# Graph kernel with rows gathered one tile at a time: the first four chunks of the first convolution gather raw rows of x in the prologue

## The chip, the cores and the metric

The kernel runs on one core of a Trainium2 chip. The metric is the time of one execution on the device in microseconds (us). Before the change three runs gave 4202.74, 4210.86 and 4212.08, so the median is 4210.86 us. The profile is of a further execution of the same kernel.

## What is computed

The reference normalizes the rows of x (12,500 rows of 256 numbers), runs two graph convolutions over 200,000 edges sorted by their destination, adds the result to x, and then runs an attention layer (its edges' first 12,500 only). What matters here is the first convolution:

```python
edge_index = jnp.stack([src, dst])
h = jnp.maximum(_layernorm(x, axis=-1), 0.0)
...
    h = x @ W_pre + b_pre
    h = _gcn_conv(h, W1, b1, src, dst, n)      # with a loop added at each node
...
    deg = jax.ops.segment_sum(ones, dst, num_segments=n)
    dinv = jnp.where(deg > 0, jax.lax.rsqrt(deg), 0.0)
    norm = dinv[src] * dinv[dst]
    msgs = h[src] * norm[:, None]
    out = jax.ops.segment_sum(msgs, dst, num_segments=n)
```

So each edge takes the row of its source, normalized and multiplied by the source's dinv, and adds it to its destination. The linear maps are applied after the sums.

## The kernel before

All of it is in `fast_path` (L414 on). Instructions stand on each engine in the order of the program, and each engine works through its own queue in that order; a buffer that is used again brings a wait for its last reader.

**The prologue** (L518 to L925) has three jobs. It counts the edges of each node on TensorE (16 blocks s = 0 to 15 in the loop at L862; `count_block` L764 makes one-hots `hot_r` on VectorE, `place` L782 and `norms` L817 turn the counts of one of five parts into `dinv`). It turns the edge lists (`turn_to`, `turn_src`). And it makes table1 in DRAM, 14 groups of 7 tiles of 128 rows: `load_x` (L575) loads a group of x on SP's queue, `stats` (L751) takes its means and variances on VectorE, and `scale(g)` (L828) multiplies the factors with four small GpSimd instructions (L834 to L837), normalizes the seven tiles on ScalarE (L846, in the last two groups partly on VectorE, L842 and L844) and stores the group to table1 (L848, SP's queue). All 14 groups have a buffer each: 11 are loaded at once, and 3 when the edge lists' memory is given back after s = 2. `scale(g)` is put into the loop when the `dinv` of its part is there.

**The first convolution** is `convolve` (L986), called at L1247. The edges are cut into 112 chunks of 14 tiles of 128 edges (the last chunk has 9 tiles): 1,563 tiles. Per tile GpSimd issues one indirect DMA that gathers 128 rows of table1 into a slice of `fgot` (L1179), and TensorE multiplies the tile with a one-hot of the destinations (L1187; two matmul instructions in the profile per tile). Per chunk VectorE makes the one-hots (`fhot`, L1073), ScalarE copies the sums out (L1103), TensorE turns them (L1038), and VectorE adds them to a sliding buffer (L1120). Finished windows of 128 nodes go through the combined weight (L1220, L1221), ScalarE (L1225) and a store to table2 (L1226). `fgot` has four buffers, so GpSimd may be four chunks ahead of TensorE. A list of due steps (`at`, `run`) places the later steps between the tiles: the first finished window ends at tile 50, in chunk 3, and brings with it `load_late` (L970), `first_chunk` (L959) and `check_chunks` (L933), whose instructions on VectorE and TensorE stand there in the queues.

**The second convolution** (L1392) does the same with table2. Its first chunk gathers from all of table2 but the last two windows (`some`, L1178), and those two are added by other means (`late_sums` L1083). Then comes **the attention** (L1399 on).

Of the kernel before, what the change touches and what calls it, by code (L numbers as in the profile page):

```python
# [413 lines left out]
def fast_path(  # L414
# [102 lines left out]

    with tc.tile_pool(name="fprep", bufs=1) as prep:  # L518
# [42 lines left out]

        dst_r = load_edges(dst, NOWHERE, "fdst_r")

# [9 lines left out]
        xs = []  # L573

        def load_x(g, pool):  # L575
            n0, n1 = g * G * P, min((g + 1) * G * P, N)

            xt = pool.tile([P, G, D1], F32, name="fxt", bufs=XB if g < XB else NG - XB)
# [10 lines left out]
        XB = 11  # L589
        for g in range(XB):  # L590
            load_x(g, prep)
            if g == 1:
                src_r = load_edges(src, 0, "fsrc_r")


        zeros = prep.tile([1, 512], BF16, name="zeros")
# [11 lines left out]
        for k in range(NPT):  # L608
# [4 lines left out]
        iota_a = prep.tile([I, L, max(AW)], BF16, name="iota_a")  # L613
        nc.gpsimd.iota(iota_a, pattern=[[0, L], [1, max(AW)]], base=0, channel_multiplier=0,
                       allow_small_or_imprecise_dtypes=True)


        sel = prep.tile([2 * R, P // LB, P], F32, name="sel")
        nc.gpsimd.memset(sel, 0.0)
        for r0, base, keep in ((0, 0, [-1, LB - 1]), (R, LB, [1, -LB])):  # L620
            s = sel[r0:r0 + R]
            nc.gpsimd.affine_select(out=s, in_=s, compare_op=ALU.not_equal, fill=1.0, base=base,
# [20 lines left out]
        for k, q in enumerate(Q):  # L643
            nc.gpsimd.tensor_mul(low_q[k], low[:, :, None].to_broadcast([NCH, J, q]),
                                 by_kq[:, k, None, :q].to_broadcast([NCH, J, q]))
        base = prep.tile([NCH, 1], F32, name="base")
        nc.vector.tensor_copy(base, dst_r[:, 0:1])
        near_t = prep.tile([P, J, NCH], BF16, name="near_t")
# [6 lines left out]
        def offsets():  # L655


            mean = prep.tile([NCH, 1], F32, name="fmean")
            nc.gpsimd.iota(mean, pattern=[[0, 1]], base=-LAG, channel_multiplier=M,
                           allow_small_or_imprecise_dtypes=True)  # L660
            nc.gpsimd.tensor_scalar(mean, mean, 0.0, None, op0=ALU.max)
            mean_i = prep.tile([NCH, 1], I32, name="mean_i")
            nc.gpsimd.tensor_copy(mean_i, mean)
            nc.vector.tensor_scalar(mean_i, mean_i, ~(P - 1), None, op0=ALU.bitwise_and)
# [39 lines left out]
        with tc.tile_pool(name="fpsum", bufs=2, space=PSUM) as psum, \  # L704
# [28 lines left out]
            def turn_to():  # L733
                to_f = rows_p.tile([NCH, CE], F32, name="fto_f")
# [3 lines left out]
            def turn_src():  # L738
                src_f = rows_p.tile([NCH, CE], F32, name="near_f")
# [42 lines left out]
            def place(k):  # L782
# [4 lines left out]
                hot = prep.tile([I, L * max(AW)], BF16, name="hot_n", bufs=2)  # L787
# [39 lines left out]

            def scale(both):  # L828
# [4 lines left out]
                flip(g)  # L833
                nc.gpsimd.tensor_mul(sc[:, ws], sc[:, ws], dinv[:, ws])  # L834
# [21 lines left out]
            def one_more():  # L856
                nonlocal n_stats
                if n_stats < NG:
                    stats(n_stats)
                    n_stats += 1  # L860

            for s, (k, j0) in enumerate(blocks):  # L862
                count_block(k, j0)
                if to_scale and to_scale[0] + 1 < n_stats:
# [15 lines left out]
                if s == 2:  # L880
# [3 lines left out]
                    for g in range(XB, NG):  # L884
                        load_x(g, more)
            place(late)
            due.append((len(blocks), late))
# [6 lines left out]
            while to_scale:  # L894
                scale(True)
            nc.vector.reciprocal(dinv2, deg)
# [36 lines left out]
    def check_chunks(work, psum):  # L933
# [9 lines left out]
        pt = psum.tile([P, KC + 1, P], F32, name="fpt", bufs=1)  # L943
# [42 lines left out]
    def convolve(ep, table, stride, width, ahead, with_sum, psum, prepare, finish, lacking=False):  # L986
# [95 lines left out]

        def late_sums():  # L1083
# [3 lines left out]
            froms = ep.tile([P, J, stride], F32, name="fgot", bufs=ahead)  # L1087
# [81 lines left out]
        hots = {0: hot_of(0)}  # L1169
# [377 lines left out]
```

## Time and profile before

| what | us |
|---|---|
| median of three runs | 4210.86 |
| the profiled execution: its time | 4207.15 |
| its span, from the first to the last instruction | 4205.4 |
| prologue: start to GpSimd's first gather from table1 | 0 to 124.5 |
| first convolution's gathers (1,563) | 124.5 to 2079.2 |
| second convolution's gathers (1,563) | 2082.4 to 4040.6 |
| attention, to the end | 4040.6 to 4205.4 |

In a row of the page's groups the name before the arrow is what is written and the name behind it what is read; then come the count, the busy time, the mean of one in ns, and the idle time of that engine just before, with what ended most of it. A row of the timeline has the start, the duration, the engine, the line and operation, and in brackets the idle time before it. In a row of waits, the engine and its line come first, then what it waited for, and then the total, the number and the longest wait. The GpSimd engine is called POOL, VectorE DVE, ScalarE ACT, TensorE PE; "issue" is time in which the engine waited for nothing that the profile shows.

### The profile page before, as it was taken

Reading aid. Unit: us, or ns where it says so; the run is one execution under the profiler, and the core shown is the slowest. Engines: PE = TensorE matmul, PEld = TensorE weight load, DVE = VectorE, ACT = ScalarE, POOL = GpSimd, SP = SyncE. Lnnn points to the kernel's source line nnn. Section 1 sums busy time; section 2 is a strip of 40 time slices with the busy share of each in tenths; the row PEclk is TensorE's granted clock in tenths of the full one; section 3 lists DMA queues with packets and bytes.
Section 4 is the critical chain, followed back from the end, with each engine's and each line's share of the span. In section 5 each row is a group of like instructions: output and inputs, shape, how many; then the busy total and the mean of one; then the engine's idle time right before and its main releaser. Section 6 shows DMA issues by size and latency. Waiting matters only on the chain. (4 is left out here: it accounts for less than half of the span.)

```text
span 4205.4 us, 31693 instructions
## 1 busy us (share of the span) xinstructions
PE 3105.7 (74%) x10423; PEld 1964.0 (47%) x10423; DVE 1098.5 (26%) x2260; ACT 459.4 (11%) x1155; POOL 3101.1 (74%) x3346
## 2 busy tenths in 40 slices
PE   6488878788787877888667777777677677777773
PEld 5254434444444444444355555555455445545552
DVE  7321111211111112111132222222222222222238
ACT  5100000000000000000001111111111111111122
POOL 3677777777777777777777777777777777777766
PEclk7687787877877778777788888888888888788877
DMA  6544444444444444444445554545555545555556
GB/s 220 156 122 120 120 120 122 120 120 120 122 119 119 119 122 119 120 119 121 128 137 140 130 127 127 132 127 128 128 132 128 128 127 132 127 127 127 132 159 203
DMA packets 326197, 551.36 MB, mean 131 GB/s; under 512 B 96041, under 2 KB 224520, under 8 KB 326024
## 3 DMA queue, kind: packets, MB, share of 16 engines
q0 software_dynamic: 153520, 414.27, 38.3%
q1 hardware_dynamic: 126966, 118.80, 9.5%
q10 hardware_dynamic: 45538, 16.17, 1.5%
q8 instruction: 86, 1.41, 0.1%
q14 instruction: 87, 0.71, 0.1%
HBM read 495.73 MB, written 53.19 MB: 131 GB/s over the span
## 5 line engine op out<-in xcount | busy, mean ns | idle before, releaser
L1179 POOL DMA_INDIRECT fgot<-ftable,fsrc_t x3112 | 2945.8, 947 | 957.2 <-issue 899.6
L1187 PE MATMUL facc<-fgot,fhot 128*128 128x257 f32 (+1 forms) x6252 | 2368.0, 499 | 912.8 <-DMA fgot<-ftable,fsrc_t 879.7
L1187 PEld LDWEIGHTS facc<-fgot,fhot 128*128 128x128 f32 x6252 | 1269.0, 233 | 1850.8 <-DMA fgot<-ftable,fsrc_t 1395.6
L1120 DVE TENSOR_TENSOR buf<-buf,fturn 128x256 f32 x224 | 94.4, 422 | 1722.9 <-PE fturn L1038 1354.3
L1073 DVE TENSOR_TENSOR fhot<-iota_p,to_t 128x1792 f32<-128x1792 f32 x224 | 448.6, 2004 | 4.3 <-PE fpt L1094 4.3
L1276 DVE SCALAR_TENSOR_TENSOR fy<-rb,fb2c,fpz 128x128 f32<-128x128 f32 x194 | 58.7, 344 | 752.3 <-PE fpz L1269 751.3
L1103 ACT ACTIVATE fsums<-facc 128x257 f32<-128x257 f32 (+1 forms) x224 | 86.1, 384 | 1236.5 <-PE facc L1187 1228.9
L1290 DVE SCALAR_TENSOR_TENSOR fx<-fpo,fdinv,fxb 128x256 f32<-128x256 f32 x97 | 46.9, 483 | 471.8 <-PE fpo L1285 471.8
L1220 PE MATMUL fpo<-wf,buf 128*128 128x256 f32 x388 | 157.1, 549 | 0.4 <-DVE buf L1120 0.4
L1225 ACT ACTIVATE fo<-fpo,fdinv 128x256 f32<-128x256 f32 x97 | 46.0, 474 | 784.9 <-PE fpo L1221 784.9
L1220 PEld LDWEIGHTS fpo<-wf,buf 128*128 128x128 f32 x388 | 115.5, 298 | 30.2 <-DVE buf L1120 0.7
L1269 PE MATMUL fpz<-buf,fwb 128*128 128x128 f32 x776 | 122.8, 310 | 0.0
L1269 PEld LDWEIGHTS fpz<-buf,fwb 128*128 128x128 f32 x776 | 120.1, 233 | 2.2 <-DVE fy L1276 0.3
L1038 PE MATMUL fturn<-fident,self 128*128 128x128 f32 x396 | 85.9, 303 | 40.0 <-DMA self<-ftable 36.4
L1285 PE MATMUL fpo<-fwo,fz 128*128 128x256 f32 x388 | 115.3, 423 | 0.0
L1456 POOL DMA_INDIRECT fal<-table_l,fsrc_t x84 | 81.7, 972 | 25.6 <-issue 22.9
L1038 PE MATMUL fturn<-fident,fsums 128*128 128x128 f32 x448 | 96.7, 302 | 0.5 <-ACT fsums L1103 0.5
L1446 PE MATMUL fends<-rows,hot_t 128*128 128x260 f32 x168 | 61.3, 511 | 42.7 <-ACT fxg L1448 40.5
L1315 ACT ACTIVATE ht<-fpt 128x256 f32<-128x256 f32 x97 | 37.3, 384 | 476.3 <-PE fpt L1311 476.3
L1221 PE MATMUL fpo<-bb,fins 2*128 2x256 f32 x194 | 85.7, 528 | 0.0
L1038 PEld LDWEIGHTS fturn<-fident,fsums 128*128 128x128 f32 x448 | 70.8, 158 | 31.6 <-issue 8.6
L1038 PEld LDWEIGHTS fturn<-fident,self 128*128 128x128 f32 x396 | 56.8, 160 | 48.3 <-issue 38.3
(225 smaller groups left out, 1555.1 us busy)
## 6 DMA issues: line engine op xcount, KB each, us to landing
fgot<-ftable,fsrc_t POOLq DMA_INDIRECT x3112, 2.8
ftable<-fxt SPq DMA_DIRECT2D x14, 910.0 KB
self<-ftable SPq DMA_DIRECT2D x99, 128.0 KB
self<-ftable SPq DMA_DIRECT2D x97, 130.0 KB
ftable<-fo ACTq DMA_DIRECT2D x98, 128.0 KB
kept_x<-fx SPq DMA_DIRECT2D x98, 128.0 KB
fxb<-in_x_dram SPq DMA_DIRECT2D x97, 128.0 KB
fxt<-in_x_dram SPq DMA_DIRECT2D x13, 896.0 KB
```

The source lines that it names most:

```text
L1038: nc.tensor.transpose(v["pt"][:, i * KC + k, :], rows[:, k * P:(k + 1) * P], ident)
L1073: nc.vector.tensor_tensor(h, iota_p[:, None, :].to_broadcast([P, n, P]), to[:, :, None].to_broadcast([P, n, P]), ALU.is_equal)
L1103: nc.scalar.activation(sb, acc, AF.Copy)
L1120: nc.vector.tensor_add(b, b, v["pt"][:, :KC, :])
L1179: nc.gpsimd.indirect_dma_start(out=got, out_offset=None, in_=table[:(NT - TW) * P, :] if some else table[:], in_offset=bass.IndirectOffset ...
L1187: nc.tensor.matmul(acc, hots[c][:, j, :], got[:, :width], start=(j == 0), stop=(j == nj[c] - 1 and not some))
L1220: nc.tensor.matmul(po, buf[:, k, :P], wf[:, k, :], start=(k == 0), stop=False)
L1221: nc.tensor.matmul(po, fs, bb, start=False, stop=True)
L1269: nc.tensor.matmul(pz[:, m, :], wb[:, k, m * P:(m + 1) * P], buf[:, k, :P], start=(k == 0), stop=(k == KC - 1))
L1285: nc.tensor.matmul(po, v["z"][:, m, :], wo[:, m, :], start=(m == 0), stop=(m == KC - 1))
L1446: nc.tensor.matmul(px, hot_t[c][:, j * P:(j + 1) * P], rows[c], start=True, stop=True)
L1456: nc.gpsimd.indirect_dma_start(out=al[:, i, :], out_offset=None, in_=(table_l if c else table_e)[:], in_offset=bass.IndirectOffsetOnAxis(a ...
```

## The change

The first four chunks of the first convolution no longer gather from table1. Their 56 gathers take raw rows of x and stand in the prologue's GpSimd queue: four, then two, then three after each block s = 0 to 15 (`fetch`). For that the first 7,168 source numbers are loaded and turned ahead of everything else, and they are split into a low and a high part and stored to DRAM (`lohi`). The four chunks are normalized in place in their `fgot` buffers: `raw_stats` takes the statistics of the 14 tiles, `raw_sources` finds the dinv of each row's source by products of one-hots with dinv (as three bf16 parts), and `raw_scaled` applies both with ScalarE. Chunk 0 is done at the end of the prologue, chunks 1 to 3 inside `convolve`, each between the chunk before it and its own matmuls (`raw_begin` at tile 3 of the chunk before, `raw_end` after its close).

The `fgot` buffers of the first convolution are five instead of four, in a pool that is opened ahead of the prologue: four hold the raw chunks, and chunk 4 is the first to gather from table1. To make room, x passes through seven buffers instead of 14: `refill` in `scale(g)`, g = 1 to 7, loads group g + 6 into the buffer of group g - 1, and its GpSimd memset stands ahead of the four GpSimd instructions of `scale(g)`. Smaller moves: `mean` is computed earlier, `sel` in two halves after blocks 1 and 2, and in the second convolution the pool with its `fgot` is opened after the work pool, so that it lies elsewhere. The attention's early tiles (`ap`) are allocated after the first convolution instead of before it.

```diff
@@ -515,6 +515,76 @@
...
+    RAW = 4
...
+    lohi = dram.tile([2, KR, P], BF16, name="lohi")
...
+    ring = ctx.enter_context(ExitStack())
+    gp = ring.enter_context(tc.tile_pool(name="fgots", bufs=1))
+    d_src = gp.tile([P, KR], F32, name="d_src")
+    raw_mv = gp.tile([P, KR, 2], F32, name="raw_mv")
+    raw_sc = gp.tile([P, KR], F32, name="raw_sc")
+    raw_st = gp.tile([P, J, 6], F32, name="raw_st")
+    parts_d = gp.tile([P, 3, NT], BF16, name="parts_d")
...
+    def new_got():
+        return gp.tile([P, J, D1], F32, name="fgot", bufs=RAW + 1)
+
+    raw = [new_got() for c in range(RAW)]
...
+    def raw_stats(c):
+
+        for j in range(J):
+            nc.vector.bn_stats(raw_st[:, j, :], raw[c][:, j, :D])
+        for j in range(J):
+            nc.vector.bn_aggr(raw_mv[:, c * J + j, :], raw_st[:, j, :])
+        k = slice(c * J, (c + 1) * J)
+        nc.scalar.activation(raw_sc[:, k], raw_mv[:, k, 1], AF.Sqrt, bias=eps)
...
+    def raw_ends(c, both):
+
+        lo, hi = both[:, :CE], both[:NT, CE:2 * CE]
+        for v, n, i in ((lo, P, 0), (hi, NT, 1)):
+            nc.sync.dma_start(v, lohi[i, c * J:(c + 1) * J, :].rearrange(
+                "t p -> (t p)").partition_broadcast(n))
+        return lo, hi
...
+    def raw_hots(ends):
+        nc.vector.tensor_scalar(ends[0], ends[0], lane, None, op0=ALU.is_equal)
+
+    def raw_sources(c, ends, m, new_psum):
+
+        lo, hi = ends
+        for j0 in range(0, J, 4):
+            j1 = min(j0 + 4, J)
+            e = slice(j0 * P, j1 * P)
+            pt = new_psum()[:NT, :(j1 - j0) * P]
+            for i in range(3):
+                nc.tensor.matmul(pt, parts_d[:, i, :], lo[:, e], start=(i == 0), stop=(i == 2))
+            nc.vector.scalar_tensor_tensor(m[:NT, e], hi[:, e], lane[:NT], pt,
+                                           op0=ALU.is_equal, op1=ALU.mult)
+        pd = new_psum()[:, :J]
+        for j in range(J):
+            nc.tensor.matmul(pd[:, j:j + 1], m[:NT, j * P:(j + 1) * P], one, start=True,
+                             stop=True)
+        nc.vector.tensor_copy(d_src[:, c * J:(c + 1) * J], pd)
...
+    def raw_scaled(c):
+
+        k = slice(c * J, (c + 1) * J)
+        nc.vector.reciprocal(raw_sc[:, k], raw_sc[:, k])
+        nc.vector.tensor_mul(raw_sc[:, k], raw_sc[:, k], d_src[:, k])
+        nc.vector.scalar_tensor_tensor(raw_mv[:, k, 0], raw_mv[:, k, 0], -1.0, raw_sc[:, k],
+                                       op0=ALU.mult, op1=ALU.mult)
+        nc.vector.tensor_copy(raw[c][:, :, D], d_src[:, k])
+        for j in range(J):
+            v = raw[c][:, j, :D]
+            i = c * J + j
+            nc.scalar.activation(v, v, AF.Relu, bias=raw_mv[:, i, 0:1], scale=raw_sc[:, i:i + 1])
...
+        early_t = rows_p.tile([KR, 5 * P], F32, name="early")
+        early_i = early_t.bitcast(I32)
+        src_e, lo_e, hi_e = (early_i[:KR, i * P:(i + 1) * P] for i in range(3))
+        nc.scalar.dma_start(src_e, src[:KR * P].rearrange("(t p) -> t p", p=P))
...
+        nc.vector.tensor_copy(src_ef, src_e)
+        raw_i = prep.tile([P, KR], I32, name="raw_i")
+        with tc.tile_pool(name="epsum", bufs=1, space=PSUM) as psum:
+            pe = psum.tile([P, KR], F32, name="fe")
+            nc.tensor.transpose(pe, src_ef, ident[:KR, :KR])
+            nc.vector.tensor_copy(raw_i, pe)
...
+        nc.scalar.dma_start(lohi.rearrange("i t p -> t i p"), early_b)
...
+        def fetch(n):
+            nonlocal fetched
+            for k in range(fetched, min(fetched + n, KR)):
+                c, j = divmod(k, J)
+                nc.gpsimd.indirect_dma_start(
+                    out=raw[c][:, j, :D], out_offset=None, in_=x[:],
+                    in_offset=bass.IndirectOffsetOnAxis(ap=raw_i[:, k:k + 1], axis=0))
+            fetched = min(fetched + n, KR)
...
@@ -571,11 +671,15 @@
...
         xs = []
-
-        def load_x(g, pool):
+        XB, XM = 4, 3
+
+        def load_x():
+            g = len(xs)
             n0, n1 = g * G * P, min((g + 1) * G * P, N)
 
-            xt = pool.tile([P, G, D1], F32, name="fxt", bufs=XB if g < XB else NG - XB)
+            low = g % (XB + XM) < XB
+            pool = prep if low else more
+            xt = pool.tile([P, G, D1], F32, name="fxt", bufs=XB if low else XM)
...
-        XB = 11
         for g in range(XB):
-            load_x(g, prep)
+            load_x()
...
+        mean = prep.tile([NCH, 1], F32, name="fmean")
+        nc.gpsimd.iota(mean, pattern=[[0, 1]], base=-LAG, channel_multiplier=M,
                        allow_small_or_imprecise_dtypes=True)
+        nc.gpsimd.tensor_scalar(mean, mean, 0.0, None, op0=ALU.max)
+        mean_i = prep.tile([NCH, 1], I32, name="mean_i")
+        nc.gpsimd.tensor_copy(mean_i, mean)
+        fetch(4)
...
+        def selects(r0, base, keep):
             s = sel[r0:r0 + R]
+            nc.gpsimd.memset(s, 0.0)
...
+        nc.vector.tensor_scalar(mean_i, mean_i, ~(P - 1), None, op0=ALU.bitwise_and)
+        fetch(2)
...
@@ -825,12 +935,19 @@
 
...
+            def refill(g):
+                if XB + XM <= len(xs) < NG:
+                    assert len(xs) < g + XB + XM
+                    load_x()
+
             def scale(both):
 
                 g = to_scale.pop(0)
                 t = xs[g]
                 ws = slice(g * G, (g + 1) * G)
                 flip(g)
+                if g:
+                    refill(g)
...
             for s, (k, j0) in enumerate(blocks):
                 count_block(k, j0)
+                if s in (1, 2):
+                    selects(*((0, 0, [-1, LB - 1]), (R, LB, [1, -LB]))[s - 1])
                 if to_scale and to_scale[0] + 1 < n_stats:
                     scale(False)
                 if s % 2 == 0:
@@ -881,9 +1000,13 @@
                     turn_src()
                     edges.close()
                     more = edges.enter_context(tc.tile_pool(name="fmore", bufs=1))
-                    for g in range(XB, NG):
-                        load_x(g, more)
+                    for g in range(XM):
+                        load_x()
+                fetch(3)
             place(late)
+            fetch(KR)
+            lohi_0 = raw_ends(0, prep.tile([P, R * BLOCK], BF16, name="hot_r", bufs=2))
+            raw_stats(0)
...
@@ -893,6 +1016,17 @@
                     norms(due.pop(0)[1])
             while to_scale:
                 scale(True)
+
+            rest = prep.tile([P, NT], F32, name="fdeg2")
+            nc.vector.tensor_copy(parts_d[:, 0, :], dinv)
+            nc.vector.tensor_sub(rest, dinv, parts_d[:, 0, :])
+            nc.vector.tensor_copy(parts_d[:, 1, :], rest)
+            nc.vector.tensor_sub(rest, rest, parts_d[:, 1, :])
+            nc.vector.tensor_copy(parts_d[:, 2, :], rest)
+            raw_hots(lohi_0)
+            raw_sources(0, lohi_0, iota_r.rearrange("p r b -> p (r b)").bitcast(F32),
+                        lambda: psum.tile([P, 4 * P], F32, name="ft"))
+            raw_scaled(0)
             nc.vector.reciprocal(dinv2, deg)
         edges.close()
...
@@ -1167,19 +1307,44 @@
...
+        def raw_begin(c):
+            if c < len(raw):
+                raw_load(c + 1)
+                raw_hots(raw_lohi[c])
+                raw_stats(c)
+
+        def raw_end(c):
+            if c < len(raw):
+                raw_sources(c, raw_lohi[c], work.tile([P, CE], F32, name="fsources", bufs=1),
+                            lambda: psum.tile([P, 4, P], F32, name="fpt", bufs=1).rearrange(
+                                "p a b -> p (a b)"))
+                raw_scaled(c)
...
+        if raw:
+            raw_load(1)
...
             if j == 0:
-                gots = ep.tile([P, J, stride], F32, name="fgot", bufs=ahead)
+                gots = raw[c] if c < len(raw) else new_rows_of()
             got = gots[:, j, :]
             some = lacking and c == 0
-            nc.gpsimd.indirect_dma_start(
-                out=got, out_offset=None, in_=table[:(NT - TW) * P, :] if some else table[:],
-                in_offset=bass.IndirectOffsetOnAxis(
-                    ap=src_0[:, j:j + 1] if some else src_t[:, c, j:j + 1], axis=0))
+            if c < len(raw):
+                if j == 3:
+                    raw_begin(c + 1)
+            else:
+                nc.gpsimd.indirect_dma_start(
+                    out=got, out_offset=None, in_=table[:(NT - TW) * P, :] if some else table[:],
+                    in_offset=bass.IndirectOffsetOnAxis(
+                        ap=src_0[:, j:j + 1] if some else src_t[:, c, j:j + 1], axis=0))
             if j == 2 and some:
                 late = late_sums()
...
             if j == nj[c] - 1:
                 close(c, acc, t)
+                if c < len(raw):
+                    raw_end(c + 1)
...
@@ -1231,6 +1398,13 @@
...
+    with tc.tile_pool(name="psum1", bufs=1, space=PSUM) as psum, \
+            tc.tile_pool(name="edges1", bufs=1) as ep, \
+            tc.tile_pool(name="fwork1", bufs=2) as work:
+        convolve(ep, table1, D1, D + 1, 4, True, psum, lambda w: prepare1(work, w),
+                 lambda w, b, s, pre, _: finish1(work, psum, w, b, s, pre), raw=raw)
+    ring.close()
...
-    with tc.tile_pool(name="psum1", bufs=1, space=PSUM) as psum, \
-            tc.tile_pool(name="edges1", bufs=1) as ep, \
-            tc.tile_pool(name="fwork1", bufs=2) as work:
-        convolve(ep, table1, D1, D + 1, 4, True, psum, lambda w: prepare1(work, w),
-                 lambda w, b, s, pre, _: finish1(work, psum, w, b, s, pre))
...
     with tc.tile_pool(name="psum2", bufs=1, space=PSUM) as psum, \
-            tc.tile_pool(name="edges2", bufs=1) as ep, \
-            tc.tile_pool(name="fwork2", bufs=2) as work:
+            tc.tile_pool(name="fwork2", bufs=2) as work, \
+            tc.tile_pool(name="edges2", bufs=1) as ep:
```

## The prediction

> **What bounds the kernel now.** I read the groups first, then GpSimd's waits, then the timeline where its stream starts and where it passes from one convolution to the other.
>
> The costliest group, from the page:
>
> ```profile
> L1179 POOL DMA_INDIRECT fgot<-ftable,fsrc_t x3112 | 2945.8, 947 | 957.2 <-issue 899.6
> ```
>
> Almost all idle time before the gathers is "issue": 0.30 us after each 0.95 us. A gather costs 1.25 us. GpSimd's waits say the same:
>
> ```profile
> POOL fgot L1179 <- issue: 903.6, 2966, 0.3
> POOL fgot L1179 <- PE facc L1187: 34.3, 103, 3.2
> POOL fgot L1179 <- DMA roots<-root_t: 9.4, 1, 9.4
> ```
>
> 103 waits for TensorE make 34.3 us, so all but one are the same 0.3 us; the one is 3.2 us. From its first gather to the last GpSimd therefore never stands behind anyone, and a microsecond on it is a microsecond of the kernel. Its timeline:
>
> ```profile
> 124.48 1.24 POOL L1179 DMA_INDIRECT fgot<-ftable,fsrc_t  x1 [9.45 <-DMA roots<-root_t]
> ...
> 265.03 0.95 POOL L1179 DMA_INDIRECT fgot<-ftable,fsrc_t  x1 [0.30 <-issue]
> ...
> 2078.24 0.94 POOL L1179 DMA_INDIRECT fgot<-ftable,fsrc_t  x1 [0.30 <-issue]
> 2082.42 0.94 POOL L1179 DMA_INDIRECT fgot<-ftable,src  x1 [3.23 <-PE facc L1187]
> ```
>
> Tile 112, chunk 8's first, is gathered at 265.0 (124.5 + 112 x 1.25 = 264.5, plus small stretches). This is my reference point: after the change GpSimd has to be past chunk 7 earlier than 265 to win anything.
>
> TensorE has slack in the steady state, but one hole, which the lead of four chunks covers today. ScalarE's, VectorE's and TensorE's timelines:
>
> ```profile
> 189.26 0.47 ACT L1225 ACTIVATE fo<-fpo,fdinv 128x256 f32<-128x256 f32 x1 [9.26 <-PE fpo L1221]
> ...
> 198.76 0.43 DVE L982 TENSOR_TENSOR fprod<-fwg,far 128x256 f32<-128x256 f32 x1 [21.71 <-DMA far<-in_L_gnn_attn_r_dram]
> ...
> 211.23 8.69 PE L1187 MATMUL facc<-fgot,fhot 128*128 128x257 f32 x26
> ```
>
> The first window's output (189.3) starts weight loads, VectorE waits for them to 198.8, and TensorE stands behind VectorE's `check_chunks` until 211.2: 22 us after 189.3.
>
> **Part 1: removed.** 56 gathers leave the stream: 56 x 1.25 = 70 us. If GpSimd started at 124.5 as now and never waited, chunk 8 would begin at 195.
>
> **Part 2: the prologue, longer by 41 us.** GpSimd is busy for only 39.2 of the first 124.5 us, so the 70 us seem to fit in. But the queue is in order. (a) Ahead of `scale(0)` (at 50.8 now) stand 27 gathers: 33.8 us. With its own work in the queue (iota_a 1.5, sel 7, low_q 2.9, the offsets about 5) from 7.5 us on, that is 57.7. The second half of sel waits for earlier gathers to land (2.8 us in the page). And VectorE's bf16 one-hots hold GpSimd up:
>
> ```profile
> 71.00 1.99 DVE L770 TENSOR_TENSOR hot_r<-near_t,iota_r 128x3360 bf16<-128x3360 bf16 x1 [1.49 <-PE tiles L778]
> 71.03 2.01 POOL L837 COPY fxt<-fdinv 128x7 f32<-128x7 f32 x1
> ...
> 2097.23 1.21 DVE L1369 TENSOR_SCALAR hot_t<-to_all,base_b,lane 128x1792 f32<-128x1792 int32 x1 [12.58 <-DMA to_all<-in_dst_dram]
> 2097.43 1.83 POOL L1179 DMA_INDIRECT fgot<-ftable,src  x1 [0.30 <-issue]
> ```
>
> A copy of 0.2 us lasts as long as the one-hot; a gather beside a VectorE operation of 1.21 us grew by 0.88, two others by 0.33 and 1.21. The Trainium skill ("SBUF — State Buffer", section "SBUF: two separate sides") is stricter: while VectorE runs such an operation GpSimd is locked out[...]. Six one-hots of 2 us fall in this stretch: 12 us by the rule, about 5 by the rows. I take the rows: `scale(0)` at 65 us (58 with no hold-up, 72 by the rule).
>
> (b) From there the seven buffers rule. The memset of `refill` in `scale(g)` waits for the store of group g - 1 to land, and GpSimd's queue (gathers, the factors) stands behind it, as ScalarE and SP's store do behind the factors. On SP's queue the refill's load stands ahead of that store and waits for the same landing; on ScalarE's queue the later parts of the count stand behind the normalizations, with a cycle's time to spare. One cycle: factors 0.95, ScalarE 7 x 0.507 = 3.55, store about 0.4 issue, 0.6 start, 2.65 data at 350 GB/s, and about 1 to be seen (the last store was issued at 117.6, data ended near 122.6, SP went on at 123.55, two stores in line): 9.2, with gathers in the same DMA engines 10. The 3 or 6 gathers of a cycle (3.8 or 7.5 us) hide in it. Seven cycles: `scale(7)` at 65 + 70 = 135, ScalarE in it at 136, against 94.7 now. The tail of six groups behind it took to 117.5, 22.8 us; x of group 13 lands at about 139 and its statistics fit in. The prologue's last normalization ends at 159.
>
> The moved `mean` frees VectorE of a wait of 5.4 us (block 4), the weights' loads move behind `lohi` on ScalarE's queue and TensorE's first work comes about 4 us later; together nothing, both hidden by (a).
>
> **Part 3: TensorE's start, another 13 us.** Now it is 19.1 us from 117.5 to the first matmul (136.6). Between them chunk 0's chain is put in on VectorE and TensorE, ahead of the roots and the first `self` loads: parts of dinv 5 x 0.2; hots 1.1 (by L735, 1792 wide, 1.15); four rounds of three bf16 matmuls of 512 columns (0.3 each by L709) and one VectorE operation (0.76, by the slope of L1276 and L1290) with two hand-overs of 0.2, 2.0 each; 14 f32 matmuls of one column, 28 instructions of 0.17 (L814: 0.12 to 0.22), 4.8; five small operations 1.1. 16, less 3 for overlap. The first matmul stands at 159 + 19 + 13 = 191, not 137. GpSimd's table is there at about 166; it gathers chunk 4 and then waits: chunk 5 needs chunk 0's buffer.
>
> **Part 4: raw chunks on TensorE, to 288.** Chunk 0: 9.4 us (28 matmuls, as the 30 in 9.38 at 136.6 now): 200. For each of chunks 1 to 3 nothing overlaps: rounds 7.5, the small matmuls 4.8, hand-overs and factors 2, then ScalarE 14 x 0.507 = 7.1, which paces the matmuls, and their end 0.7: about 21.5 (18 with a warm TensorE, 23 with a cold one). VectorE's 14 statistics (4.7 + 1.1) and one-hots lie beside. 200 + 64.5 = 265. Then the hole: tile 50 is in chunk 3, `fo` stands behind chunk 3's 14 normalizations on ScalarE, TensorE behind `check_chunks`: 22 us plus the last matmuls, 23 more. Its cover, the lead of four chunks, is gone. Chunk 3's buffer is free at 288, and chunk 8 waits for it. 288 against 265: **+23 us**. The 70 us have turned into waits for TensorE. Behind it TensorE makes a chunk in about 10 us against GpSimd's 17.5, and no wait is left.
>
> **Part 5: the passage to the second convolution, +10.** In the changed order of instructions its first gather waits for the last store of table2 (its `fgot` now lies on the `fo` buffers), no longer for the last matmul. That store was issued at 2090.0 and SP went on at 2092.05; GpSimd began at 2082.4. So 9.7 to 10 us; not below zero, since that store can't land before the last matmul. The first chunk without the last two windows then buys nothing.
>
> The five buffers, the lower DMA traffic of the first convolution and the moved attention tiles I cost at nothing: GpSimd's stream hides them, and VectorE and SP wait for that same store in both kernels.
>
> **Sum.** +23 + 10 = +33 us on the profiled execution: 4207 + 33 = 4240. That execution lies 3.7 us under the median, so 4244 against the median.
>
> **The rivals.** *No hold at the memset (not slower):* stores land before GpSimd comes to the memset, and a cycle costs only its three gathers and the factors, 3.8 + 0.95 = 4.7 us. Price: 7 x 5.3 = 37 us off my sum, 4207 for the median. All else as worked out, it decides at a cycle of 5.3 us (33 / 7 = 4.7 below 10). With raw chunks of 18 us as well, 10 more, it is faster: 4197. For it speaks that GpSimd has 85 idle us in the prologue; against it stand the instruction order, where the memset waits for the store just issued, and ScalarE's 3.55 us in each cycle. *Half of it:* cycles of 7.5 us, chunks of 19: 18 + 8 us less: 4218, near no change. *GpSimd starves:* the one-hots stop every gather wholly and gathers land slowly under loads and stores, so that cycles last 13 us: 21 more, 4265; for it the lock-out rule, against it that most of the stretch falls into time in which GpSimd waits for the store anyway. The full gain, 70 us less the passage's 10, would need TensorE to take four raw chunks for nothing; the hole at 189 us speaks against it, and I give it no chance of its own.
>
> **How the numbers follow.** About 0.2%, 8 us, is what the measurement can tell from no change. My sum 0.62 (4226 to 4260 by the ends of its terms), starving 0.14, half 0.10 (in equal parts slower and same), no hold 0.14 (0.08 faster, 0.06 same). Slower by over 0.2% 0.81, within it 0.11, faster 0.08. Range 4212 to 4268: the low end leaves out the case of no hold, the high end takes in starving.
>
> **What would show it.** After: `scale` memsets waiting for table1's stores, some 10 us apart; the first gather of table1 near 166; the first matmul near 190; then waits of `fgot` for `facc` of about 17, 4, 4 and 27 us, and chunk 8 near 288; a wait of about 13 us at the passage. I am wrong if the memsets pass without a wait, if chunk 8 begins before 255, or if a raw chunk takes under 15 us.

## The result and the profile after

The changed kernel takes 4246.67 us (median of 4 runs, 4243.86 to 4250.75) against 4209.35 us for the kernel before (4 runs; the median of the first three was 4210.86): ratio 1.0092, 95% interval 1.0074 to 1.0109. It is slower by 37 us. The profiled execution took 4243.86 us with a span of 4242.0 us; the one of before had 4205.4, so the two traces differ by 36.6 us.

GpSimd's gathers are still the costliest group. From the page of the changed kernel, busy time and mean ns of one behind the first bar, idle time behind the second:

```profile
L1344 POOL DMA_INDIRECT fgot<-ftable,fsrc_t x3056 | 2891.4, 946 | 988.3 <-issue 893.3
...
L659 POOL DMA_INDIRECT fgot<-in_x_dram,raw_i x56 | 72.0, 1287 | 15.6 <-issue 15.4
```

56 gathers left the first group, and with them 54 us of busy time; its idle time grew by 31 us. The second group holds the same 56, now from x, and each takes 1287 ns where one from table1 takes 946. The waits of GpSimd in the changed kernel (total us, times, longest):

```profile
POOL fgot L1344 <- issue: 897.3, 2913, 9.9
POOL fgot L1344 <- PE facc L1352: 76.7, 96, 26.0
...
POOL fxt L683 <- DMA ftable<-fxt: 20.1, 5, 5.6
...
POOL fgot L1344 <- DMA ftable<-fo: 14.6, 1, 14.6
```

Before, the waits for facc made 34 us and none was over 3.2. Three things are new: a wait of up to 26.0 us for TensorE, 20.1 us of memsets that wait for stores of table1, and 14.6 us for a store of table2. GpSimd's timeline of the changed kernel shows where they lie; the first five lines are the first gathers of chunks 4 to 8, the last is the first gather of table2:

```profile
177.17 1.04 POOL L1344 DMA_INDIRECT fgot<-ftable,fsrc_t  x1 [9.88 <-issue]
...
206.94 0.94 POOL L1344 DMA_INDIRECT fgot<-ftable,fsrc_t  x1 [12.47 <-PE facc L1352]
...
228.36 0.94 POOL L1344 DMA_INDIRECT fgot<-ftable,fsrc_t  x1 [4.20 <-PE facc L1352]
...
251.57 0.94 POOL L1344 DMA_INDIRECT fgot<-ftable,fsrc_t  x1 [6.00 <-PE facc L1352]
...
294.78 0.95 POOL L1344 DMA_INDIRECT fgot<-ftable,fsrc_t  x1 [26.01 <-PE facc L1352]
...
2123.60 0.94 POOL L1344 DMA_INDIRECT fgot<-ftable,src  x1 [14.64 <-DMA ftable<-fo]
```

Chunk 8 begins at 294.8 and not at 265.0: 29.8 us late, although 70 us of gathers are gone. Table2 begins at 2123.6 and not at 2082.4: 41.2 us late, 11.4 of them new. The first gather of the mixing (the attention's last step, L1625 here and L1456 before) stands at 4098.3 and not at 4061.2, 37.1 late: the wait in front of it, for the last windows' `table_l`, is 9.7 us in place of 13.1. So the difference of the spans is 30 at the start, 11 at the passage, and 4 given back ahead of the mixing.

The hole that the lead covered before the change lies open. ScalarE's, VectorE's and TensorE's timelines of the changed kernel:

```profile
270.73 0.45 ACT L1392 ACTIVATE fo<-fpo,fdinv 128x256 f32<-128x256 f32 x1
...
277.84 0.42 DVE L1116 TENSOR_TENSOR fprod<-fwg,far 128x256 f32<-128x256 f32 x1 [12.03 <-DMA far<-in_L_gnn_attn_r_dram]
...
289.99 8.28 PE L1352 MATMUL facc<-fgot,fhot 128*128 128x257 f32 x26
```

TensorE's last matmuls of chunk 3 end at 272.2. But for three small ones of `check_chunks` it stands until 290.0, while VectorE waits for weights and works through `check_chunks`, and GpSimd stands behind it.

### The profile page after: what moved, and what is told of

Its sections match the earlier page's. It is cut to its first block, busy times and chain, and to the rows that moved or that the text cites. A ratio compares the mean times of both kernels' runs of the same rounds, so it can differ in the third digit from the quotient of the medians.

```text
span 4242.0 us, 32286 instructions
## 1 busy us (share of the span) xinstructions
PE 3105.4 (73%) x10584; PEld 1986.1 (47%) x10584; DVE 1141.1 (27%) x2424; ACT 488.2 (12%) x1215; POOL 3118.9 (74%) x3347
## 5 line engine op out<-in xcount | busy, mean ns | idle before, releaser
L1344 POOL DMA_INDIRECT fgot<-ftable,fsrc_t x3056 | 2891.4, 946 | 988.3 <-issue 893.3
L1352 PE MATMUL facc<-fgot,fhot 128*128 128x257 f32 (+1 forms) x6252 | 2341.9, 496 | 892.9 <-DMA fgot<-ftable,fsrc_t 854.2
L1445 DVE SCALAR_TENSOR_TENSOR fy<-rb,fb2c,fpz 128x128 f32<-128x128 f32 x194 | 58.8, 344 | 747.8 <-PE fpz L1438 746.8
L1625 POOL DMA_INDIRECT fal<-table_l,fsrc_t x84 | 81.6, 971 | 25.6 <-issue 23.2
L659 POOL DMA_INDIRECT fgot<-in_x_dram,raw_i x56 | 72.0, 1287 | 15.6 <-issue 15.4
```

What stands on the lines that cost most here:

```text
L659: nc.gpsimd.indirect_dma_start(out=raw[c][:, j, :D], out_offset=None, in_=x[:], in_offset=bass.IndirectOffsetOnAxis(ap=raw_i[:, k:k + 1], ...
L1344: nc.gpsimd.indirect_dma_start(out=got, out_offset=None, in_=table[:(NT - TW) * P, :] if some else table[:], in_offset=bass.IndirectOffset ...
L1352: nc.tensor.matmul(acc, hots[c][:, j, :], got[:, :width], start=(j == 0), stop=(j == nj[c] - 1 and not some))
L1625: nc.gpsimd.indirect_dma_start(out=al[:, i, :], out_offset=None, in_=(table_l if c else table_e)[:], in_offset=bass.IndirectOffsetOnAxis(a ...
```

## The experiments

The theory: the 70 us saved on GpSimd's stream are eaten by (A) a longer prologue, where in-order queues wait for the store just issued and bf16 one-hots hold up the gathers, (B) TensorE's serial raw chunks, (C) the hole at window 0, no longer covered, and (D) the passage. The rivals: one of these alone, or DMA traffic.

The runs e1 to e4 and e9 to e12 came from two chips on which TensorE was granted a clock of 0.71 to 0.72 (0.78 to 0.80 in the other runs). The kernel before takes 4956 to 4958 us there. In the traces of these eight GpSimd stands about 5 us in every 40 all through the steady state, so a gain on its stream need not reach the end, and their ratios are known only to some 12 us to either side. They are read by where GpSimd stands at the start, against runs of the same set.

**e1: gather buffers clear of the fo tiles.**

```diff
-            tc.tile_pool(name="edges1", bufs=1) as ep, \
-            tc.tile_pool(name="fwork1", bufs=2) as work:
+            tc.tile_pool(name="fwork1", bufs=2) as work, \
+            tc.tile_pool(name="edges1", bufs=1) as ep:
...
-            tc.tile_pool(name="edges2", bufs=1) as ep:
+            tc.tile_pool(name="edges2", bufs=1) as ep, \
+            tc.tile_pool(name="fgots2", bufs=1) as gots2:
```

`lohi_t` and `fsources` move to `ep`, and conv2's `fgot` to the pool `gots2`.

> The changed kernel with its memory laid out so that the second convolution's gather buffers no longer lie on anything of the first convolution's work pool (the fo tiles): the first gather of table2 then waits for the last matmuls of the first convolution again, as in the kernel before, and not for the last store of table2. Theory (the passage costs 11 us because of that store): the wait of 14.6 us at the passage falls to about 3, GpSimd's gathers of table2 start 11 us earlier, and the kernel takes 4236 us. Rival (the work behind the passage waits for that store anyway, since the last rows of table2 are needed soon, so that the wait only moves on): a new wait of about 11 us shows up within the first chunks of table2, and the time stays at 4247 us.

Measured: 4988.09 us, ratio 1.0073 (1.0047 to 1.0099). The first gather of table2 waits for `PE facc` as meant, but for 36.7 us, because TensorE is behind on this chip. It settles nothing on the 11 us; e6 does.

**e2: the late loads at window 8.**

```diff
-            if w == 0:
+            if w == 8:
                 load_late(work)
```

> The changed kernel with load_late, first_chunk and check_chunks done at window 8 in place of window 0. Theory (the raw chunks take the lead of four chunks that covers this hole before the change): TensorE goes on at about 272 instead of 290, GpSimd's wait for facc ahead of chunk 8 falls from 26 us to about 6, at window 8 the gathers are far ahead again and no new wait appears; 4247 - 20 = 4227 us. Rival (the hole is hidden under TensorE's serial work on chunk 3, or comes back at window 8): the wait of 26 us stays above 20, or a new one of the same size appears near window 8, and the time stays within 4243 to 4247 us.

Measured: 4990.63 us, ratio 1.0059 (1.0034 to 1.0083). Table1's first gather stands at 180.5 here and at 180.8 in e1, so the two can be compared. Chunk 8's first gather in e1, and then in e2:

```profile
310.02 0.95 POOL L1344 DMA_INDIRECT fgot<-ftable,fsrc_t  x1 [28.39 <-PE facc L1352]
```

```profile
293.36 0.95 POOL L1344 DMA_INDIRECT fgot<-ftable,fsrc_t  x1 [8.45 <-PE facc L1352]
```

The wait shrinks by 19.9 us and chunk 8 comes 16.7 earlier. (C) is there with its size. That it reaches the end could not be seen on this chip.

**e3: each refill one group later.**

```diff
-                if g:
+                if g > 1:
                     refill(g)
```

> The changed kernel with each refill of a buffer of x one group later, so that the memset and the load wait for the store of the group before last, which has had a cycle to land. Theory (the in-order queues of GpSimd and SP behind the store just issued set the cycle of scale): the five memset waits (20.1 us together) vanish, the seven cycles fall from 10.9 to about 8 us (gathers and factors), the prologue ends 20 us earlier, and the kernel takes 4227 us. Rival (VectorE's hold-up of the gathers and the DMA traffic set the cycle, the memset waits only fill what is left): the gathers take up the freed time, scale(7) starts at 140 or later, and the kernel takes 4241 to 4247 us.

Measured: 4992.58 us, ratio 1.0068 (1.0044 to 1.0093). The memset waits, in e1 and then in e3:

```profile
POOL fxt L683 <- DMA ftable<-fxt: 21.0, 5, 5.6
```

```profile
POOL fxt L683 <- DMA ftable<-fxt: 3.4, 1, 3.4
```

ScalarE begins `scale(0)` at 71.3 and `scale(7)` at 132.0, 8.7 us a cycle; in e1 it is 73.3 and 150.2, 11.0 a cycle. Table1's first gather comes at 162.3 against 180.8, chunk 8 at 294.6 against 310.0. The in-order wait is part of (A).

**e4: the seven buffers alone.**

```diff
-    raw = [new_got() for c in range(RAW)]
+    raw = []
...
-                fetch(3)
```

and so on: no gather from x, no raw chain.

> The changed kernel without the gathers from x and without all that makes them into chunks: x still passes through seven buffers, all chunks are gathered from table1 into five buffers, and the order of the pools is the changed one. Theory (the seven buffers alone make cycles of about 9.5 us, scale(0) is back near 51): scale(7) starts near 117, the prologue's last normalization ends near 140 instead of 117.5, no wait for facc follows since the lead is back, and the passage still costs 11; 4210 + 22 + 11 = 4243 us. Rival (it is the 56 gathers in GpSimd's queue that make the prologue long, and stores land in time without them): the prologue ends by 125 and the kernel takes 4221 to 4228 us.

Measured: 4992.74 us, ratio 1.0079 (1.0058 to 1.0100). GpSimd's waits in e4, and its first gather of table1:

```profile
POOL fxt L683 <- DMA ftable<-fxt: 57.0, 7, 8.7
```

```profile
151.73 1.24 POOL L1330 DMA_INDIRECT fgot<-ftable,fsrc_t  x1 [9.18 <-DMA self<-ftable]
```

With no raw gather at all each memset waits 8.1 us, and ScalarE's `scale(0)` at 51.7 and `scale(7)` at 122.2 are 10.1 us a cycle. Table1 starts 27 us later than before the change (124.5). So the buffers alone account for about half of the 52.7 us by which the changed kernel's table1 starts late. Against e1, which starts 29.1 us later than e4, the other half is 21.6 us ahead of `scale(0)` (73.3 against 51.7), where the 27 gathers stand, and 6.4 in the seven cycles (11.0 against 10.1): the gathers between the scales hide nearly wholly in waits that are there without them.

**e5: the changed kernel again.**

> The changed kernel once more, beside the three that follow. Where GpSimd's gathers set the pace (1.25 us each without a wait in the steady state) every theory expects the 36 us of the first measurement again: 4247 us against 4210. Where TensorE is granted a lower clock and sets the pace, the kernel before took 4958 us in the first set of runs, and the changed one should lie 30 to 37 us above it, since its TensorE starts on table1's chunks that much later.

Measured: 4242.49 us, ratio 1.0088 (1.0072 to 1.0105), on a chip with the clock at 0.80. Table1 starts at 170.6 and chunk 8 at 285.5; the profiled execution is 9 us under the median.

**e6: the three edits together.**

> The changed kernel with three edits together: refills one group later, load_late and its checks at window 8, and the gather buffers of the second convolution clear of the fo tiles. Theory (the three costs lie one behind the other on GpSimd's stream): chunk 8's first gather comes 16 us earlier for the refills and 17 us earlier for the hole than without them, near 262 instead of 294.5, which is the 265 of the kernel before, and the wait at the passage is back at 3 us: 4204 to 4210 us where gathers set the pace, that is 40 us under the changed kernel and no measurable gain over the kernel before, because every gather taken out of the stream stands in GpSimd's prologue instead. Rival (TensorE's serial raw chunks take up what the refills give): chunk 8 at 275 or later and 4217 us or more.

Measured: 4199.63 us, ratio to before 0.9984 (0.9977 to 0.9991): 43 us under e5 on the same chip, of the expected 40. In e6's timeline of GpSimd the starts of table1, of chunk 8 and of table2:

```profile
163.29 1.04 POOL L1344 DMA_INDIRECT fgot<-ftable,fsrc_t  x1 [9.86 <-issue]
...
259.46 0.94 POOL L1344 DMA_INDIRECT fgot<-ftable,fsrc_t  x1 [4.29 <-PE facc L1352]
...
2077.53 0.94 POOL L1344 DMA_INDIRECT fgot<-ftable,src  x1 [4.18 <-PE facc L1352]
```

In e5 they are 170.6, 285.5 with a wait of 26.6, and a wait of 14.1 for the store of `fo`. So 7 us are the refills', 19 the hole's, 10 the passage's, and 4 are lost again ahead of the mixing: 32, as the two spans differ (4231.3 and 4198.8); the medians differ by more since the profiled e5 ran 9 us under its own. (A), (C) and (D) add up along GpSimd's stream, and the rival of e6 is out. What is left of (B) is seen too: chunks 5 to 8 still wait 14.2, 4.0, 4.5 and 4.3 us for facc, 27 us. With three costs mended, 70 us of gathers taken out of the stream are worth 6 us, 0.15%.

**e7: two raw chunks, gathers where GpSimd is idle.** On top of e6, with `RAW = 2`:

```diff
-                fetch(3)
+                if s < 3:
+                    fetch(3)
...
             while to_scale:
                 scale(True)
+            fetch(KR)
```

> As the last one, but only the first two chunks are raw (five buffers all the same), and their 28 gathers are placed where GpSimd is idle: 15 ahead of the second half of sel, and 13 behind the factors of the last group, under ScalarE's last normalizations. Theory (gathers cost the kernel only where they stand ahead of a scale): scale(0) is back near 52, cycles take 6 us, the first gather of table1 comes near 140, chunk 8 near 245, and the kernel takes 4189 us, 20 under the kernel before. Rival (the passage of x through seven buffers sets the prologue whatever is in the queue, as in the run with the buffers alone, whose first gather of table1 came at 152): first gather near 152, chunk 8 near 257, 4201 us or more.

Measured: 4185.35 us, ratio to before 0.9954 (0.9937 to 0.9970): 20 us faster than the kernel before, the best at this clock. From e7's timeline, the start of table1 and of chunk 8:

```profile
139.60 0.94 POOL L1345 DMA_INDIRECT fgot<-ftable,fsrc_t  x1 [0.30 <-issue]
...
244.75 0.95 POOL L1345 DMA_INDIRECT fgot<-ftable,fsrc_t  x1 [0.30 <-PE facc L1353]
```

Chunk 8 begins 20.2 us earlier than before the change (265.0), which is what the end gains. Table1's gathers follow those from x without a gap, and no wait for facc is over 3.7 us. GpSimd begins `scale(0)` at 55.8, ScalarE's `scale(0)` and `scale(7)` stand at 56.7 and 102.6, a cycle of 6.6 us; the memsets wait 21.3 us in these cycles all the same, so there the stores' way through the seven buffers holds GpSimd up, and not its gathers.

**e8: a bf16 operation beside the gathers.**

```diff
             one_hots(h[:, :n, :], to_0 if lacking and c == 0 else to_t[:, c, :n])
+            if with_sum and c > 20:
+                nc.vector.tensor_tensor(extra[:, 0, :], extra[:, 1, :], extra[:, 2, :],
+                                        ALU.is_equal)
```

> The changed kernel with one extra VectorE operation behind each one-hot of the first convolution from chunk 21 on: is_equal of two bf16 tiles of 128x3360 into a third, the size of the counting's one-hots, whose result nobody reads. It measures VectorE's hold-up of GpSimd by itself, in the steady state where a gather takes 0.95 us and f32 one-hots of 2.0 us lie beside it without a trace. If bf16 operations shut GpSimd's descriptor writing out wholly, each stretches the gather it meets by its whole length, about 2 us, and 91 of them make the gathers' stream up to 180 us longer (less where TensorE sets the pace). If they only slow it in part, as the rows I took in the prediction say (0.33 to 0.88 us), about 40 to 70 us. If the stretch in the prologue came from elsewhere (loads and stores on the DMA engines), nothing.

Measured: 4366.84 us in one run. One of the 91, between ordinary gathers, in e8's timeline:

```profile
1010.36 0.95 POOL L1350 DMA_INDIRECT fgot<-ftable,fsrc_t  x1 [0.30 <-issue]
...
1010.76 2.00 DVE L1211 TENSOR_TENSOR fhot<-iota_p,to_t 128x1792 f32<-128x1792 f32 x1
1011.61 0.94 POOL L1350 DMA_INDIRECT fgot<-ftable,fsrc_t  x1 [0.30 <-issue]
...
1012.69 1.89 DVE L1220 TENSOR_TENSOR extra<-extra 128x3360 bf16<-128x3360 bf16 x1
1012.86 2.54 POOL L1350 DMA_INDIRECT fgot<-ftable,fsrc_t  x1 [0.30 <-issue]
```

The f32 one-hot of 2.00 us leaves the gather beside it at 0.94. The bf16 operation of 1.89 us makes it 2.54: the gather ends at 1015.40, 0.82 us after the operation (1014.58). So do all the others: each of the 91 operations of this trace stretches one gather, and all 91 of these end 0.82 or 0.83 us after their operation. The hold lasts to the operation's end, as in the first of the three cases. Against e5's median the 91 still cost 124 us, 1.37 each and not 1.89, since part of an operation often passes before a gather is held: a gather that had begun 0.27 us before the operation was held, and one that had begun 0.31 us before it was not. A held gather grows by 0.8 to 2.0 us, according to when it began.

The two operations differ in their type and in where an operand lies (`iota_p` is in PSUM, both inputs of `extra` are in SBUF). bf16 is not needed for the hold: an operation on int32 and f32, both in SBUF, does the same (L746, shown under part 2(a)). No run changed the place alone.

**e9 and e10: e2 and e3 once more.**

> The move of load_late and its checks to window 8 alone, once more, beside the next three, because the first time came from a chip on which TensorE was granted a lower clock and set the pace. Theory (the hole is on GpSimd's stream once the raw chunks have eaten the lead): chunk 8 comes 17 to 20 us earlier and so does the end, 4243 - 18 = 4225 us. Rival (TensorE makes up for the hole elsewhere): 4240 us or more.

> The refills one group later alone, once more, for the same reason. Theory (the prologue ends earlier by what the memset waits cost, all of it on the path): 16 us earlier at chunk 8 and at the end, 4227 us. By the run with all three edits, whose prologue gained only 7 us over the unchanged order on the same chip (first gather of table1 at 163.3 against 170.6), it is less: 4235 us. Rival (nothing reaches the end, since TensorE's raw chunks pace the start): 4241 us or more.

Measured: 4974.50 us, ratio 1.0036 (1.0014 to 1.0058), and 4978.26, ratio 1.0040 (1.0018 to 1.0063). The lower clock again: the single edits' worth at the end stays unmeasured, only their sum is shown by e6. The starts add something. The wait ahead of chunk 8 is 9.0 us in e9 and 27.2 in e10, so the hole goes with e2's edit a second time. Over the six traces with four raw chunks and the refill order of the change, table1 starts at 170.6, 174.7, 177.2, 177.2, 180.5 and 180.8; over the three with later refills at 162.3, 163.3 and 166.8. The means are 12.7 us apart, and single pairs say anything from 4 to 18: one trace of a start is good to some 10 us only.

**e11: e4 with the three edits.**

> The run with the buffers alone (no gathers from x, no raw chunks, seven buffers, chunks gathered from table1 into five buffers), with the same three edits. Theory (the seven buffers still cost some us in the prologue, and no gather leaves the stream): the first gather of table1 comes near 134, ten us later than before the change, no wait follows, 4206 + 10 = 4216 us. It shows what the 28 raw gathers of the run with two raw chunks are worth: 4216 - 4185 = 31 us, near 28 x 1.25 = 35. Rival (later refills make seven buffers cost nothing): 4206 us, and the raw gathers are worth 21.

Measured: 4980.53 us, ratio 1.0043 (1.0024 to 1.0063). Table1's first gather comes at 132.8, 8.3 us later than before the change: by this one trace, that is what the seven buffers cost with later refills. At 17.5 us a chunk its chunk 8 would begin at 272.8, if nothing held it (at this clock it comes at 288.4, after waits); e7's begins at 244.8. By this estimate, across two chips, the 28 raw gathers of e7 are worth 28 us, their 35 less the 7 by which table1 starts later. It fits the 20 us that e7 gains on the kernel before, with 8 for the buffers.

**e12: three raw chunks.**

```diff
-                fetch(3)
+                fetch(3 if s < 3 else 2 if s >= 6 and fetched < 29 else 0)
```

> Three raw chunks: 15 gathers ahead of the second half of sel, 14 or so by twos behind the factors of a group, where GpSimd waits for the next memset anyway (30 us of waits in the run with two raw chunks), 13 behind the last factors. Theory (these 14 hide wholly, and TensorE's third raw chunk ends before its buffer is asked for): first gather of table1 near 140 as with two, chunk 8 near 227, 17.5 us less than with two, 4168 us. Rival (each stretches under VectorE's bf16 one-hots or delays the next scale, or TensorE's serial chain is now the bound): chunk 8 at 238 or later, 4179 us or more.

Measured: 4965.37 us, ratio 1.0027 (1.0002 to 1.0052). GpSimd's start of table1 and its first wait in e12, with a row of TensorE and one of VectorE between them:

```profile
137.76 4.37 PE L571 MATMUL ft<-fone,iota_r 98*128 98x1 f32 x28 [0.33 <-DVE iota_r L567]
...
146.26 0.95 POOL L1344 DMA_INDIRECT fgot<-ftable,fsrc_t  x1 [0.30 <-issue]
...
148.77 0.17 DVE L573 COPY d_src<-ft 128x14 f32<-128x14 f32 x1 [10.68 <-remote]
...
199.17 0.94 POOL L1344 DMA_INDIRECT fgot<-ftable,fsrc_t  x1 [18.24 <-PE facc L1352]
```

Table1 starts 13.5 us later than in e11, which ran on the same chip with no raw gather at all: 3.7 of them lie ahead of ScalarE's `scale(0)` (56.3 against 52.6), 1.7 in the seven cycles (52.9 against 51.2), and 8.0 behind the last normalization, where 13 gathers stand in a row (14.2 to table1's first gather against 6.2). So the 12 that stand between the scales hide nearly wholly.

Then chunk 5 waits 18.2 us for chunk 0, and the next two 10.4 and 9.9. This looks like the rival (TensorE's chain is the bound), but it does not show it. TensorE's first facc matmul stands at 190.9, 58.8 us behind the last normalization; in the other runs with raw chunks, on chips of both kinds, that way takes 28.2 to 31.3. Pauses lie in it: VectorE copies the result of TensorE's small matmuls 6.6 us after their end (142.1 to 148.8), where e7 has both at 135.5. The trace names no releaser of this core for them ("remote"). Chunk 8 comes at 271.3, and whether three raw chunks beat two at a clock of 0.80 was not seen.

## Why the prediction was right

The mechanism was the forecast's in every part, and the size nearly so: 4244 forecast, 4246.67 measured; +33 us of span, +36.6 measured. The near hit hides terms that were off in both directions: the prologue came 11 us later than forecast and the passage 1.4, TensorE's start gave 4 back and the mixing 3.4. That they nearly cancel is luck.

**Part 1, removed: right.** 56 gathers of 1.25 us left the stream. Where their new place is idle and nothing waits for TensorE, as in e7, 28 of them bring some 28 us (an estimate, worked out under e11).

**Part 2(a), ahead of `scale(0)`: mis-sized.** I had 65, with 5 us for VectorE's hold-up; GpSimd begins `scale(0)` at 70.0. The 27 gathers ahead of it take 10.9 us more than 27 x 0.95. Two of them, from the timelines of GpSimd and VectorE in the changed kernel, beside VectorE operations whose inputs both lie in SBUF:

```profile
8.45 2.02 DVE L746 TENSOR_TENSOR near_f<-fdst_r,low 112x1792 f32<-112x1792 int32 x1
...
9.66 1.64 POOL L659 DMA_INDIRECT fgot<-in_x_dram,raw_i  x1 [0.30 <-issue]
...
43.42 1.70 DVE L899 TENSOR_TENSOR hot_n<-a_bf,iota_a 56x1526 bf16<-56x1526 bf16 x1
...
43.90 5.93 POOL L659 DMA_INDIRECT fgot<-in_x_dram,raw_i  x1 [0.30 <-issue]
...
45.05 3.94 DVE L880 TENSOR_TENSOR hot_r<-near_t,iota_r 128x3584 bf16<-128x3584 bf16 x2
```

The first ends at 11.30, 0.83 us after VectorE's operation (10.47), the second at 49.83, 0.84 after the last of three one-hots (48.99). The row that I had leaned on says the same: the gather of 1.83 ends at 2099.26, 0.82 after its operation (2098.44). I had taken its growth of 0.88 for the price of an operation; it came out so small because the gather had begun 0.20 us after its operation. So the mistake was in the reading of the rows, and the rule that I had set against them (the Trainium skill, "SBUF — State Buffer", section "SBUF: two separate sides": an operation with two inputs in SBUF shuts GpSimd out for its whole length, if GpSimd reads SBUF) fits the traces. It gave 72 and was nearer. e8 shows the hold alone, and what it costs a stream on average.

**Part 2(b), the cycles: 1 us short each.** They are 10.9 us long in place of 10 (`scale(0)` at 70.0, `scale(7)` at 146.1), and five of the seven memsets wait, as said of all. Two of them, from GpSimd's timeline of the changed kernel:

```profile
89.48 0.12 POOL L683 MEMSET fxt<- 128x28 f32 x1 [5.16 <-DMA ftable<-fxt]
...
123.73 0.12 POOL L683 MEMSET fxt<- 128x28 f32 x1 [5.63 <-DMA ftable<-fxt]
```

e4 has 10.1 without any gather, so the 10 of the sum is right for the store's way. The rest lies in two cycles, of 13.7 and 12.2 us on ScalarE. In the first of them one-hots run beside the factors themselves (L953 takes 3.73 us and L954 1.51, in place of 0.25 and 0.19); what made the other long was not taken apart. e3 takes most of the wait away and the cycle falls to 8.7. The tail, from ScalarE's `scale(7)` to its last normalization, was forecast at 22.8 us and measures 22.8 (147.0 to 169.8). (a) and (b) together make the prologue 11 us later than forecast.

**Part 3, TensorE's start: 4 us too much.** 28.2 us from the last normalization to the first facc matmul (169.8 to 198.0), where 32 were forecast.

**Part 4, the raw chunks and the hole: right.** Chunk 0 took 8.7 us (9.4), chunks 1 to 3 took 65.5 (64.5; the terms listed for one chunk add up to 22.1 and not to 21.5, and the three measure 21.4, 23.2 and 20.9), and from there, 272.2, to chunk 8's gather it was 22.6 (23). The waits forecast at 17, 4, 4 and 27 us are 12.5, 4.2, 6.0 and 26.0. Chunk 8 was due at 288 and came at 294.8: 11 late from the prologue, 4 of it regained at TensorE's start.

**Part 5, the passage: right.** 11.4 us against 10; moving the buffers takes it away (e6).

**A term left out.** Ahead of the mixing 3.4 us come back: GpSimd waits there for the last windows in either case, and less when it comes later. Without it the changed kernel would have stood some 40 us behind and not 37, against 33 forecast.

Of the rivals, the case of no hold at the memset fell with the 20.1 us of waits. "GpSimd starves" had a right cause, the lock-out, and half of its size: 11 us in the prologue (5 ahead of `scale(0)`, 6 in the cycles), not 21. That one cause alone accounts for the loss is ruled out by e6, in which three edits at three places each return their part. What the traffic on the DMA engines adds to the stores' landing was not taken apart.

## What to carry to other kernels

Work that is moved into an idle stretch of an in-order queue is free only where nothing behind it in that queue is urgent: 27 gathers ahead of the scales put them 21.6 us back (e1 against e4), 12 between the scales cost 1.7 us (e12 against e11), and 13 in a row behind the last one 8 of their 16 us. When buffers are recycled, let the refill wait for the store before last, not for the one just issued (the waits fell from 21.0 to 3.4 us in e3). And before a lead is spent, list what it was covering: here it was a hole of 20 us in a step that the change does not touch.

## What was not expected of the hardware

A gather on GpSimd that begins beside VectorE's bf16 is_equal of 128x3360 (1.89 us, both inputs in SBUF) ends 0.82 or 0.83 us after it, 91 times out of 91 in e8, in place of taking 0.95. An f32 one-hot of 2.00 us, one operand of which lies in PSUM, leaves the gather at 0.94.

The granted TensorE clock was not the same from chip to chip: 0.78 to 0.80 in the first measurement and in e5 to e8, 0.71 to 0.72 on two other chips, where the kernel before took 4958 and 4956 us in place of 4206 to 4209. There GpSimd, which never waits in the steady state at the higher clock, stands about 5 us in every 40, once in two chunks. From e1's timeline:

```profile
349.94 0.94 POOL L1344 DMA_INDIRECT fgot<-ftable,fsrc_t  x1 [4.92 <-remote]
...
390.10 0.94 POOL L1344 DMA_INDIRECT fgot<-ftable,fsrc_t  x1 [5.39 <-remote]
```

The trace names no releaser of this core for these waits ("remote"). What makes them stays open. Longer matmuls are not it: the 6,252 rows of facc take 437 ns on average in e1 and 496 in the changed kernel.
